# Two layers of a decoder in one program: layer 1's attentions form their scores twice, keys side by side for the maximum and keys on partitions for the exponentials

## The chip, the cores and the metric

The kernel runs on one core of one Trainium2 chip, as one program. The time is the device time of an execution in microseconds (us). A profile is one more execution, recorded by the hardware profiler; its span runs from the first to the last instruction. The engines are PE (TensorE, with its weight loads as PEld), DVE (VectorE), ACT (ScalarE), POOL (GpSimd) and SP (SyncE, which here only issues DMAs).

## The reference, cut to what matters

32 sequences of 128 tokens with 128 features pass through two layers, all in float32. Layer 0 is a recurrent (RWKV) block, a cross attention with 16 heads of 64 features over the sequence's context and 128 memory positions, and a mixture of eight experts with two chosen per token. Layer 1 is a causal self attention with normalised queries and keys ("sa" below), a windowed cross attention ("wa") and a linear layer on values rounded to blocks of four-bit floats. Each is added to the residual stream.

```python
x = x + rwkv(layernorm(x)); x = x + cross_attention(layernorm(x), ctx); x = x + experts(layernorm(x))

# layer 1, self attention: 16 heads of 8 features
q, k = headnorm(q, gq, bq), headnorm(k, gk, bk)
scores = jnp.where(causal, einsum('nhld,nhmd->nhlm', q, k), -1e30)
x = x + einsum('nhlm,nhmd->nhld', softmax(scores), v) @ Wo.T + bo

# layer 1, windowed cross attention: 16 heads of 8 features, keys and values are ctx itself
scores = einsum('bhqd,bhkd->bhqk', layernorm(x), ctx) / sqrt(8)
scores = jnp.where(abs(i - j) > 64, -inf, scores)
x = x + einsum('bhqk,bhkd->bhqd', softmax(scores), ctx) @ W_proj.T + b_proj

x = x + quantised(layernorm(x)) @ quantised(weight).T + bias
```

The masked, full softmax of a score tile is what the change forms in another way.

## The kernel before

**Work.** The 32 sequences are cut into ten groups (`SIZES`: three of two, six of four, one of two). Layer 0 works group by group; its expert layer gathers tokens into 39 blocks of 256, of which 22 are planned with layer 0 and 17 with layer 1. Layer 1 works group by group, too: a group's self attention, then its windowed attention, then its quantised linear layer, and inside an attention sequence by sequence. There are 32 + 32 such attentions of one sequence, each with 16 heads.

**Order.** Nothing is issued directly. Each operation is recorded with its engine, a weight (its estimated length in us), what it reads and writes, and a due time `at`. `Plan.run` then plays the program through as a list of events: an engine that comes free takes, of its operations that are ready and find room in their rings of buffers, the one that is due first. The order so found is written into each engine's instruction stream and stays fixed. `SHIFTS` holds, for each of the two layers, corrections to the due times by kind of operation. `SWITCH` is what the planner charges when PE changes its tiling. PE runs untiled for most work, split by rows for scores ("rows") and by columns for value sums ("columns").

**Layer 0, where the change touches it.** In `rwkv`, the eight scans of a group each need v and r repeated over partitions. For early groups (`early`, line 581) a matmul with `sel` makes each repeat (L640), and the eight products are summed in the matmuls of L694. For the others, v and r go to HBM and come back repeated by DMA (L646, L650), and POOL sums the products (L690). `clear` writes zeros to the 17 MB buffer `xreg` by DMA in the same stage. The cross attention's scores are L843, its transposes L865, its value sums L796.

**One attention of layer 1** (`attention`, L1307). Heads are stored 8 features each on 128 partitions; a row tile of 32 partitions holds four heads. POOL multiplies the keys by a mask of heads (`km`, L1311), so that one row tile's matmul gives four heads' scores side by side. PE first writes the causal or window mask into PSUM as an identity times a bf16 mask of 0 and -1e30 (L1317), then adds the scores of four row tiles (L1325). They stand with queries on partitions: two tiles `sc` of 128 x 1024, eight heads each. For each, DVE takes the negated maximum over keys (`nm`, L1338) and adds it (`e`, L1340), ACT takes exponentials (L1342), PE turns the eight heads by transposes (L1350), ACT copies them out of PSUM (`eT`, L1353). The value sums (L1358) need keys on partitions, which the transposes are for; values carry a column of ones, so that the sums of the exponentials come out beside them. ACT copies (`avs`), PE turns back (`ot`, L1369), DVE divides (L1376, L1377).

PSUM has eight banks of 128 x 512 floats: ring `big` of two pairs (scores, expert hidden values) and ring `one` of four single banks (all else), shared by both layers. The self attention of group g + 1 is planned ahead of the windowed attention of group g.

## Time and profile before

| | us |
|---|---|
| three timed executions | 1518.4, 1513.4, 1508.7; median 1513.4 |
| the profiled execution, its own time | 1505.7 |
| its span | 1504.0 |
| PE busy, share of the span | 1387.6, 92% |
| DVE busy | 1227.2, 82% |
| ACT busy | 967.9, 64% |
| POOL busy | 697.5, 46% |
| granted PE clock, mean | 0.982 |

Layer 0's attentions take about the first 815 us, the expert blocks the time to about 985, layer 1's attentions the rest. Busy time is the time in which an engine had at least one instruction under way. Matmuls are pipelined and their ends are modelled, so that a matmul's duration is longer than the time by which it delays the next one. A group of instructions stands in the profile with its source line, engine, operation, output and inputs, their shapes, the count, the total and the mean duration, and what ended the engine's idle time before it. Shares of busy time are means over stages with different limits; the prediction reads them stage by stage.

### The profile page before, as it was taken

The numbers are of one execution on the slowest core, as the hardware profiler recorded it, in microseconds if no ns is written. First come the engines' busy times: TensorE is split into PE (matmuls) and PEld (weight loads), VectorE is DVE, ScalarE is ACT, GpSimd is POOL, SyncE is SP. The second block draws the span as 40 slices with busy tenths as digits, with TensorE's granted clock in tenths as the row PEclk, the third lists the DMA queues.
The fourth block names the chain that finished last, engine by engine and source line by source line (L and its number), as shares of the span: only waits on it lengthen the run. The fifth ranks groups of instructions, "written<-read, shape, count | busy, mean of one in ns | idle before, by whom it ended". The sixth has DMA issues, their size and how long they took to land. (4 is left out here: it accounts for less than half of the span.)

```text
span 1504.0 us, 34761 instructions
## 1 busy us (share of the span) xinstructions
PE 1387.6 (92%) x12957; PEld 1069.1 (71%) x12957; DVE 1227.2 (82%) x2688; ACT 967.9 (64%) x2423; POOL 697.5 (46%) x1010
## 2 busy tenths in 40 slices
PE   6899999999999999999998998987888989999995
PEld 4678777787887878878787887964556656566664
DVE  6899898887878868796656575689999989999996
ACT  2467656676766766565674343446777888888784
POOL 6444554543546235262303466658553552553432
PEclk9999999999999999999999998999999999999997
DMA  9903030301203112020000776823000000000000
GB/s 332 324 24 108 16 123 19 113 30 66 84 1 108 43 63 86 2 79 5 16 2 24 230 210 177 252 81 88 15 12 12 19 12 12 16 8 19 5 9 18
DMA packets 80504, 107.64 MB, mean 72 GB/s; under 512 B 7152, under 2 KB 48624, under 8 KB 80336
## 3 DMA queue, kind: packets, MB, share of 16 engines
q1 hardware_dynamic: 75792, 95.97, 20.3%
q0 software_dynamic: 4544, 9.45, 1.8%
q8 instruction: 103, 1.69, 0.5%
q14 instruction: 65, 0.53, 0.1%
HBM read 73.01 MB, written 32.38 MB: 70 GB/s over the span
## 5 line engine op out<-in xcount | busy, mean ns | idle before, releaser
L855 ACT ACTIVATE e<-sc,nm 128x256 f32<-128x256 f32 x512 | 238.3, 482 | 26.1 <-DVE nm L848 26.0
L848 DVE TENSOR_REDUCE nm<-sc 128x4 f32<-128x1024 f32 x128 | 154.6, 1216 | 26.7 <-PE sc L843 25.8
L865 PE MATMUL tr<-ident,e 128*128 128x128 f32 x1024 | 144.0, 278 | 8.7 <-DVE xoT L816 7.5
L865 PEld LDWEIGHTS tr<-ident,e 128*128 128x128 f32 x1024 | 114.4, 142 | 40.6 <-issue 18.9
L1162 ACT ACTIVATE hT<-h_ps,wb 128x256 f32<-128x256 f32 x156 | 65.6, 470 | 94.2 <-PE h_ps L1159 77.4
L805 POOL COPY wide<-xrs 128x512 f32<-128x512 f32 (+1 forms) x80 | 49.0, 614 | 156.9 <-DVE xrs L803 59.9
L843 PE MATMUL sc<-xk,xq 64*128 64x128 f32 x1024 | 112.2, 296 | 0.0
L690 POOL TENSOR_TENSOR r<-r,r 128x512 f32<-128x512 f32 (+1 forms) x49 | 60.3, 1230 | 111.5 <-DVE r L688 98.7
L869 ACT COPY eT<-tr 128x512 f32<-128x512 f32 x128 | 75.3, 588 | 54.5 <-PE tr L865 50.5
L855 ACT ACTIVATION_READ_ACCUMULATOR e<-sc,nm 128x1 f32 x512 | 109.2, 213 | 0.0
L796 PE MATMUL av<-eT,xv 128*64 128x128 f32 x1024 | 104.1, 282 | 0.4 <-DVE xv L778 0.2
L1183 POOL DMA_INDIRECT ytok<-rw,bk_at x78 | 76.9, 986 | 54.5 <-DVE xT L1134 24.6
L843 PE MATMUL sc<-mkT,xq 64*128 64x128 f32 x1024 | 99.9, 272 | 0.0
L796 PE MATMUL av<-eT,mvx 128*64 128x128 f32 x1024 | 99.9, 274 | 0.0
L843 PEld LDWEIGHTS sc<-xk,xq 64*128 64x128 f32 x1024 | 77.9, 187 | 25.5 <-issue 20.7
L871 DVE COPY eT<-tr 128x512 f32<-128x512 f32 x128 | 86.1, 675 | 7.5 <-PE tr L865 7.0
L684 DVE TENSOR_TENSOR_SCAN s<-dec,v 128x512 f32<-128x512 f32 (+1 forms) x80 | 87.1, 1094 | 1.1
L766 ACT COPY xk<-xk_ps 128x512 f32<-128x512 f32 (+1 forms) x80 | 40.0, 501 | 72.3 <-PE xk_ps L764 67.5
L1340 DVE TENSOR_TENSOR e_sa<-sc_sa,nm_sa 128x1024 f32<-128x1024 f32 x64 | 78.4, 1225 | 6.9 <-ACT ff_xn L506 0.5
L816 DVE TENSOR_TENSOR xoT<-av,overs 128x512 f32<-128x512 f32 (+1 forms) x80 | 46.3, 578 | 45.7 <-PE av L796 40.2
L1340 DVE TENSOR_TENSOR e_wa<-sc_wa,nm_wa 128x1024 f32<-128x1024 f32 x64 | 78.4, 1225 | 6.2 <-DVE nm_wa L1338 0.5
L1338 DVE TENSOR_REDUCE nm_sa<-sc_sa 128x8 f32<-128x1024 f32 x64 | 77.8, 1215 | 6.3 <-PE sc_sa L1325 5.6
(586 smaller groups left out, 3932.0 us busy)
## 6 DMA issues: line engine op xcount, KB each, us to landing
xreg<-zero SPq DMA_DIRECT2D x8, 2112.0 KB
v<-spill_v SPq DMA_DIRECT2D x48, 256.0 KB
r<-spill_r SPq DMA_DIRECT2D x48, 256.0 KB
wk<-in_wexp SPq DMA_DIRECT2D x8, 512.0 KB
wq<-in_wexp SPq DMA_DIRECT2D x8, 512.0 KB
wv<-in_wexp SPq DMA_DIRECT2D x8, 512.0 KB
mkT<-in_wexp SPq DMA_DIRECT2D x8, 512.0 KB
mvx<-in_wexp SPq DMA_DIRECT2D x7, 512.0 KB
```

What stands on the lines that cost most here:

```text
L684: V(1.34, lambda u=u, s=s: vec.tensor_tensor_scan(s(), flat(dec()), u(), 0.0, ALU.mult, ALU.add), [dec, u], [s, ("scan", (g, j))])
L796: pe.matmul(av()[r, b], mvx[:, 2 * c + par] if half else v()[:, b, r], eTs[b // 2]()[:, par, half, b % 2], start=(half == 0), stop=(half = ...
L843: pe.matmul(sc()[:, par, at : at + T], q()[r, b0 + b], mkT[r, c] if half else k()[r, b0 + b], start=True, stop=True)
L848: V(1.22, lambda: vec.tensor_reduce(nm(), sc().rearrange("p j (b k) -> p j b k", k=2 * T), AX.X, ALU.max, negate=True), [sc], [nm])
L855: act.activation(e()[:, par, b], sc()[:, par, b * 2 * T : (b + 1) * 2 * T] .rearrange("p (c k) -> p c k", k=T), AF.Exp, bias=nm()[:, par, ...
L865: pe.transpose(tr()[:, half, b], e()[:, par, b, half], ident)
L869: A(0.6, lambda tr=tr: act.copy(eT()[:, 1], tr()), [tr], [(eT, 1)])
L871: V(0.68, lambda tr=tr: vec.tensor_copy(eT()[:, 0], tr()), [tr], [(eT, 0)])
L1162: A(0.47, lambda f=f: act.activation(hT()[:, f], hid(f), AF.Gelu, bias=wb()[:, f : f + 1]), [(h_ps, f % 2), wb] + ["exp"] * (j < BLK1), [( ...
L1183: d = pool.indirect_dma_start(out=ytok, out_offset=bass.IndirectOffsetOnAxis(ap=at()[:, c : c + 1], axis=0), in_=yr()[:, c], in_offset=None)
L1338: V(1.22, lambda nm=nm, sc=sc: vec.tensor_reduce(nm(), sc(), AX.X, ALU.max, negate=True), [scs[half]], [nm])
L1340: V(1.22, lambda nm=nm, sc=sc, e=e: vec.tensor_add(e(), sc(), bc(nm(), T)), [scs[half], nm], [e])
```

## The change

In layer 1, scores are formed twice. The first scores are as before, and DVE takes the negated maxima from them (`nm`, now one tile of four row tiles with 32 columns each). The maxima are split into a bf16 part and its remainder, transposed once (`nT`) and spread over four heads by a mask (`nx`, bf16). Then the scores are formed again with the keys as the stationary side, so that keys stand on partitions: a matmul of ones with `nx` writes the negative maximum into PSUM, and the keys times the masked queries (`qm`, made on ACT) are added (`st`). ACT takes the exponentials straight from PSUM into `eT`. The mask of the reference is applied after that, by POOL: `affine_select` sets the exponentials outside the causal or window region to zero. The subtraction on DVE, the sixteen transposes and the four copies are gone.

Around it, the PSUM rings belong to the layers: layer 0 keeps two pairs and four single banks, layer 1 has three pairs and two single banks. Self attentions are planned two groups ahead of the windowed ones, with four value buffers instead of three. In layer 0, group 2 is no longer early. The planner may hold PE to its present tiling: among ready operations due within `keep` of the first, one in the present mode goes first (`KEEP`, 1.3 in layer 0, none in layer 1). All shifts of due times are new.

```diff
--- before.py
+++ after.py
@@ -30,6 +30,7 @@
 assert sum(SIZES) == NB
 H, DH = 16, 8
 XH, XD = 16, 64
+VP = 32
 E, FF = 8, 512
 NF = FF // P
 NEG = -1e30
@@ -72,52 +73,45 @@
 
 
 SHIFTS = [{
-    "ACT cen#ps# cen#": 0.09, "ACT cen#ps# sq#": -0.22, "ACT g#ps# gate#": -1.15, "ACT h#ps# wb#": 0.6,
...
+    "ACT": -0.66, "ACT cen#ps# cen#": 0.78, "ACT dd#ps# dd#": -0.98, "ACT g#ps# gate#": 1.41,
...
+    "DVE xr# bk#which#": 1.05, "DVE xsm# xrs#": -0.48, "DVE xv#ps# xv#": -0.32, "KEEP": 1.3,
...
 }, {
...
 }]
@@ -150,8 +144,7 @@
     HANDOVER = {("PE", "ACT"): 0.2, ("PE", "DVE"): 0.2, ("DVE", "PE"): 0.13, ("DVE", "ACT"): 0.17,
                 ("DVE", "POOL"): 0.2, ("ACT", "DVE"): 0.07, ("ACT", "POOL"): 0.15, ("POOL", "DVE"): 0.05}
 
-
-    SWITCH, KEEP = 0.13, 0.0
+    SWITCH = 0.13
 
     def __init__(self, shifts):
         self.ops, self.seen, self.at, self.size, self.shifts = [], {}, 0.0, 1.0, shifts
@@ -194,6 +187,8 @@
         free_at = dict.fromkeys(engines, 0.0)
         room, events, order, t = {}, [], [], 0.0
         turns, modes = {}, dict.fromkeys(engines)
+
+        keep = abs(self.shifts.get("KEEP", 0.0))
         for o in self.ops:
             banks = [x for x in o[4] if x.pool.space == PSUM]
             for x in o[4]:
@@ -215,8 +210,17 @@
                 for e in engines:
                     if free_at[e] > t + 1e-9:
                         continue
-                    for k, (_, i) in enumerate(ready[e]):
+                    other = None
+                    for k, (at, i) in enumerate([*ready[e], (math.inf, None)]):
+                        if other is not None and at > ready[e][other][0] + keep:
+                            k, other = other, -1
+                            i = ready[e][k][1]
+                        if i is None:
+                            break
                         if ready_at[i] > t + 1e-9:
+                            continue
+                        change = keep and self.ops[i][7] != modes[e]
+                        if change and other is not None and other >= 0:
                             continue
                         new = {x: None for x in self.ops[i][4] if not x.held}
                         for x in list(new):
@@ -228,6 +232,9 @@
                             continue
                         if any(q in turns and max(turns[q][x] for x in xs) >= given[q] + len(xs)
                                for q, xs in need.items()):
+                            continue
+                        if change and other is None:
+                            other = k
                             continue
                         for q, xs in need.items():
                             room[q] -= len(xs)
@@ -280,13 +287,13 @@
     vec, act, pool, pe, sync = nc.vector, nc.scalar, nc.gpsimd, nc.tensor, nc.sync
 
     const = ctx.enter_context(tc.tile_pool(name="const", bufs=1))
-    ps_big = ctx.enter_context(tc.tile_pool(name="ps_big", bufs=2, space=PSUM))
-    ps_one = ctx.enter_context(tc.tile_pool(name="ps_one", bufs=4, space=PSUM))
-
     loads = []
 
 
     layer0 = ExitStack()
+    ps_big = layer0.enter_context(tc.tile_pool(name="ps_big", bufs=2, space=PSUM))
+    ps_one = layer0.enter_context(tc.tile_pool(name="ps_one", bufs=4, space=PSUM))
+    BIGS = [2, 4]
     const0 = layer0.enter_context(tc.tile_pool(name="const0", bufs=1))
 
     def load(name, shape, src, at=0.0, pool=const):
@@ -343,7 +350,12 @@
 
     hq = const.tile([P, 4], F32, tag="hq", name="hq")
     vec.tensor_reduce(hq, hm.rearrange("p (r i) -> p i r", i=4), AX.X, ALU.add)
+
+    hm8 = const.tile([P, 4], F32, tag="hm8", name="hm8")
     hqs = const.tile([P, 4], F32, tag="hqs", name="hqs")
+    vec.tensor_reduce(hm8, ident.rearrange("p (r c) -> p c r", c=VP)[:, 0:4], AX.X, ALU.add)
+    vec.tensor_reduce(hqs, ident.rearrange("p (r c) -> p c r", c=VP)[:, 4:8], AX.X, ALU.add)
+    vec.tensor_add(hm8, hm8, hqs)
     vec.tensor_scalar_mul(hqs, hq, 1.0 / math.sqrt(DH))
 
     hmp = const.tile([P, H], F32, tag="hmp", name="hmp")
@@ -450,10 +462,10 @@
         plan.op("SP", weight, fn, r, w, land)
 
     def big(name):
-        return Ring(ps_big, "big", 2, [P, 2, 512], name)
+        return Ring(ps_big, "big", BIGS[0], [P, 2, 512], name)
 
     def one(shape, name):
-        return Ring(ps_one, "one", 4, shape, name)
+        return Ring(ps_one, "one", BIGS[1], shape, name)
 
     def xk(g):
         return f"x{g}"
@@ -578,7 +590,7 @@
     def rwkv(g):
         start, n = plan.at, SIZES[g]
 
-        early = g < 3
+        early = g < 2
 
         def w(i):
             return rw[:, i, :]
@@ -1222,8 +1234,7 @@
 
     LEAD = 2
     RG = 4
-    VP = 32
-    NVX = 3
+    NVX = 4
 
     def centre_qk():
 
@@ -1236,7 +1247,7 @@
                                                   start=True, stop=True), [t], [ps2])
             V(0.2, lambda w=w, ps2=ps2: vec.tensor_copy(w, ps2()), [ps2], ["wqkv"])
 
-    vxs = []
+    vxs, nm_tiles, batches = [], [], []
 
     def pad_values():
 
@@ -1249,6 +1260,10 @@
                 pool.memset(t[:, :, :, DH : DH + 1], 1.0)
 
             G(3.0, fill, [], [f"vx16_{i}"])
+        for i in range(3):
+            t = work.tile([P, RG, VP], F32, tag=f"nmw{i}", bufs=1, name=f"nmw{i}")
+            nm_tiles.append(t)
+            G(0.3, lambda t=t: pool.memset(t, 0.0), [], [f"nmw_{i}"])
 
     def prepare_sa(g, n):
         xnT = turned(g, normal(g, "sa"), same, f"sa_xnT{g}", "xnT")
@@ -1305,11 +1320,19 @@
         return xnT, cT, hqs, vx, vkey, band
 
     def attention(m, b, qT, kT, headmask, vx, vkey, mask, o):
+
+
         n = plan.at
         plan.at = n - 1.2
-        km = wt([P, 4, T], "km", f"km{m}")
+        km, qm = (wt([P, 4, T], i, f"{i}{m}", 3) for i in ("km", "qm"))
         G(1.05, lambda: pool.tensor_mul(km(), kT()[:, b].unsqueeze(1).to_broadcast([P, 4, T]),
                                         bc(headmask, T)), [kT], [km])
+
+        def mask_q():
+            for i in range(4):
+                act.activation(qm()[:, i], qT()[:, b], AF.Copy, scale=headmask[:, i : i + 1])
+
+        A(1.4, mask_q, [qT], [qm])
         scs = [big(f"sc16_{m}_{half}") for half in range(2)]
         for half in range(2):
             def masks(half=half):
@@ -1326,31 +1349,59 @@
                           start=False, stop=True)
 
         M(0.9, scores, [qT, km], scs, "rows")
+
+        turn = len(batches)
+        batches.append(m)
+        nm, hi = turns("nm16", nm_tiles, turn), sm([P, RG, 4], "hi16", f"hi16_{m}", 3, BF16)
+        for half in range(2):
+            V(1.22, lambda half=half: vec.tensor_reduce(
+                nm()[:, 2 * half : 2 * half + 2, 0:4], scs[half]().rearrange("p j (h k) -> p j h k", k=T),
+                AX.X, ALU.max, negate=True), [scs[half]], [(nm, half)] + [f"nmw_{turn % 3}"] * (turn < 3))
+
+        def split():
+            vec.tensor_copy(hi(), nm()[:, :, 0:4])
+            vec.tensor_sub(nm()[:, :, 4:8], nm()[:, :, 0:4], hi())
+
+        V(0.4, split, [], [nm, hi])
+        nT = one([P, T], f"nT{m}")
+        M(0.14, lambda: pe.transpose(nT(), nm().rearrange("p r c -> p (r c)"), ident), [nm], [nT])
+        nx = wt([P, 4, T], "nx", f"nx{m}", 3, BF16)
+        V(0.69, lambda: vec.tensor_mul(nx(), nT().unsqueeze(1).to_broadcast([P, 4, T]), bc(hm8, T)), [nT], [nx])
+        plan.at = n - 0.5
+        sts = [big(f"st16_{m}_{half}") for half in range(2)]
+
+        def scores_turned():
+            for r in range(RG):
+                rows = slice(VP * r, VP * (r + 1))
+                pe.matmul(sts[r // 2]()[:, r % 2], ones16[rows], nx()[rows].rearrange("p h q -> p (h q)"),
+                          start=True, stop=False)
+            for r in range(RG):
+                rows = slice(VP * r, VP * (r + 1))
+                pe.matmul(sts[r // 2]()[:, r % 2], kT()[rows, b], qm()[rows].rearrange("p h q -> p (h q)"),
+                          start=False, stop=True)
+
+        M(1.15, scores_turned, [kT, qm, nx], sts, "rows")
         av = one([P, 4, T], f"av16_{m}")
         eTs = []
         for half in range(2):
-            def sc(half=half):
-                return scs[half]().rearrange("p j (h k) -> p (j h) k", k=T)
-
-            plan.at = n - 1.2
-            nm = sm([P, 8], "nm16", f"nm16_{m}_{half}")
-            e = wt([P, 8, T], "e16", f"e16_{m}_{half}", 4)
-            V(1.22, lambda nm=nm, sc=sc: vec.tensor_reduce(nm(), sc(), AX.X, ALU.max, negate=True),
-              [scs[half]], [nm])
-            V(1.22, lambda nm=nm, sc=sc, e=e: vec.tensor_add(e(), sc(), bc(nm(), T)), [scs[half], nm], [e])
-            plan.at = n - 0.5
-            A(1.06, lambda e=e: act.activation(e(), e(), AF.Exp), ["gelu"], [e])
-            eT = wt([P, 8, T], "eT16", f"eT16_{m}_{half}", 4)
+            eT = wt([P, 8, T], "eT16", f"eT16_{m}_{half}", 6)
             eTs.append(eT)
-            for j in range(2):
-                tr = one([P, 4, T], f"tr16_{m}_{half}_{j}")
-
-                def turn(j=j, tr=tr, e=e):
-                    for i in range(4):
-                        pe.transpose(tr()[:, i], e()[:, 4 * j + i], ident)
-
-                M(0.44, turn, [e], [tr])
-                A(0.6, lambda j=j, tr=tr, eT=eT: act.copy(eT()[:, 4 * j : 4 * j + 4], tr()), [tr], [(eT, j)])
+            A(1.06, lambda half=half, eT=eT: act.activation(
+                eT().rearrange("p h q -> p (h q)"), sts[half]().rearrange("p j n -> p (j n)"), AF.Exp),
+              [sts[half], "gelu"], [eT])
+
+            def select(eT=eT):
+
+                if mask is causal:
+                    pool.affine_select(out=eT(), in_=eT(), pattern=[[0, 8], [1, T]], compare_op=ALU.is_ge,
+                                       fill=0.0, base=0, channel_multiplier=-1)
+                    return
+                for q0, sign in ((0, 1), (WINDOW, -1)):
+                    part = eT()[:, :, q0 : q0 + WINDOW]
+                    pool.affine_select(out=part, in_=part, pattern=[[0, 8], [sign, WINDOW]], compare_op=ALU.is_ge,
+                                       fill=0.0, base=WINDOW + sign * q0, channel_multiplier=-sign)
+
+            G(1.1 if mask is causal else 1.3, select, [], [eT])
 
         def attend():
             for h in range(H):
@@ -1489,18 +1540,21 @@
     layer0.close()
 
     plan = Plan(SHIFTS[1])
-    with tc.tile_pool(name="small1", bufs=1) as small, tc.tile_pool(name="work1", bufs=1) as work:
+    BIGS[:] = 3, 2
+    with (tc.tile_pool(name="ps_big1", bufs=3, space=PSUM) as ps_big,
+          tc.tile_pool(name="ps_one1", bufs=2, space=PSUM) as ps_one,
+          tc.tile_pool(name="small1", bufs=1) as small, tc.tile_pool(name="work1", bufs=1) as work):
         def tiles_of(name, j, shape):
-            return wt(shape, "xT", f"xT{j}") if name == "xT" else wt(shape, "eT16", f"hT{j}", 4)
+            return wt(shape, "xT", f"xT{j}") if name == "xT" else wt(shape, "eT16", f"hT{j}", 6)
 
         BLK_AT[0] = 0.5
         for j in range(BLK1, NBLK):
             expert_block(j, -NBLK * BLK_AT[0] - 8)
         plan.at = -12
         pad_values()
-        jobs = [("sa", 0)]
+        jobs = [("sa", 0), ("sa", 1)]
         for g in range(NG):
-            jobs += [("sa", g + 1)] * (g + 1 < NG) + [("wa", g)]
+            jobs += [("sa", g + 2)] * (g + 2 < NG) + [("wa", g)]
         n = 0
         for i, (tag, g) in enumerate(jobs):
             if tag == "sa":
```


## The prediction

> **What bounds the kernel now.** I read the timeline in 40 slices first, then busy time in stretches, then the groups of instructions by shape, and last the order of time on single engines.
>
> ```profile
> PE   6899999999999999999998998987888989999995
> DVE  6899898887878868796656575689999989999996
> POOL 6444554543546235262303466658553552553432
> ```
>
> Slices are 37.6 us. Layer 0 fills the first 21, the expert blocks follow to about 985 us, and layer 1's attentions take the last 13 or so. PE is full nearly throughout; DVE is as full only in the last part.
>
> ```profile
> core 0: us, PE busy (x) PEld busy (x) DVE busy (x) ACT busy (x) POOL busy (x), PEclk, DMA share, GB/s
> 0.00:50.00 50.00, 33.27 (x139) 25.22 (x140) 35.18 (x101) 13.18 (x33) 30.19 (x73) 0.97 0.99 345
> 50.00:100.00 50.00, 47.61 (x315) 36.89 (x314) 45.79 (x112) 27.05 (x87) 18.04 (x27) 1.00 0.44 148
> ...
> 150.00:790.00 640.00, 626.31 (x6066) 502.84 (x6065) 511.81 (x1024) 422.23 (x1290) 270.42 (x360) 1.00 0.15 50
> 1280.00:1394.00 114.00, 106.22 (x1146) 72.37 (x1142) 105.48 (x167) 93.34 (x165) 52.42 (x69) 1.00 0.05 14
> ```
>
> The third row is layer 0's steady state: PE 97.9% busy, nobody else above 80%, so PE's work is its time. The fourth is 16 attentions of layer 1 in steady state (two sa groups, two wa groups, 57 us each): PE 106.2 and DVE 105.5 of 114 us. Two engines share the bound, and the chain of waits there runs mostly over DVE's maximum and subtraction. POOL has 61.6 us free.
>
> ```profile
> L1340 DVE TENSOR_TENSOR e_wa<-sc_wa,nm_wa 128x1024 f32<-128x1024 f32 x64 | 78.4, 1225 | 6.2 <-DVE nm_wa L1338 0.5
> L1338 DVE TENSOR_REDUCE nm_wa<-sc_wa 128x8 f32<-128x1024 f32 x64 | 77.8, 1216 | 3.4 <-PE sc_wa L1325 3.4
> L1353 ACT COPY eT_wa<-tr_wa 128x512 f32<-128x512 f32 x128 | 68.7, 592 | 18.8 <-PE tr_wa L1350 18.3
> L1342 ACT ACTIVATE e_wa<-e_wa 128x1024 f32<-128x1024 f32 x64 | 67.2, 1064 | 5.5 <-DVE e_wa L1340 4.9
> L1311 POOL TENSOR_TENSOR kmwa<-wa_ctxT,hqs 128x512 f32<-128x512 f32 x32 | 33.3, 1042 | 77.8 <-PE sc_sa L1325 33.8 <-issue 25.4 <-PE sc_wa L1325 18.6
> L1401 POOL TENSOR_SCALAR fx_t<-fx_t 128x512 f32<-128x512 f32 x6 | 3.7, 613 | 0.5
> ```
>
> These price an attention: two maxima and two subtractions on DVE are 2 x (1.216 + 1.225) = 4.88 us.
>
> ```profile
> 1340.91 1.04 PE L1350 MATMUL tr_sa<-ident,e_sa 128*128 128x128 f32 x8
> 1341.88 1.08 PE L1358 MATMUL av_sa<-eT_sa,vx 128*32 128x128 f32 x32
> 1342.93 0.59 PE L1317 MATMUL sc_wa<-band,ident 128*128 128x512 bf16 x2
> 1343.45 1.14 PE L1325 MATMUL sc_wa<-kmwa,wa_xnT 32*128 32x512 f32 x8
> 1344.52 0.66 PE L1369 MATMUL otsa<-ident,avssa 128*128 128x128 f32 x4
> ```
>
> On PE starts are what counts, because an end overlaps the next start. Eight transposes take 0.97 us to the next start, 0.10 of it a change from whole-array to tiled matmuls, so one costs 0.107. Two mask matmuls take 0.52, with a change, so 0.21 each. Eight score pieces take 1.07, with a change: four row tiles run side by side, 0.85 of streaming and about 0.1 for the first weights. In layer 0, four transposes stand 0.43 apart from the next block of whole-array work and 0.53 from a tiled one: again 0.10 a change.
>
> **The change, part by part.** *Layer 0, fewer repeats on PE.* Group 2 no longer repeats v and r by matmul (16 of 128x256) and sums its eight products on POOL instead of in the matmul (7 fewer). Such a matmul is two instructions, 0.43 us start to start in that stage: 23 x 0.43 = 9.9 us off PE. Added are 2 stores and 16 loads of 128 KB on SP's queue, and 7 POOL sums of 128x256 at 0.73 (the bias add of that shape), 5.1 us on an engine 42% busy. The loads queue behind the 17 MB of clearing, which keeps DMA at 0.99 of the first 50 us and is over by about 75; in the changed order group 2's projections stand among group 0's cross attention, which covers the wait. Uncovered, it is bounded by the 4 to 9 us that group 3's loads spread over now.
>
> *Layer 0, another order.* All due times are new and PE now may prefer an operation of its present tiling for up to 1.3 us. Counting tiling changes in the two instruction orders: 388 before, 307 after, 81 x 0.10 = 8.1 us. PE's 18.0 us together are worth their length only where PE is full; in the first 100 us it is 81% busy, and most of the repeats lie there. I take 16; bounds 20 and 0.
>
> *Layer 1, DVE.* Per attention the two subtractions (2.45) go. Added are a split of the 128x16 maxima in two small operations (the reciprocal of that shape has 0.24, so 0.5) and one 128x512 product out of PSUM (the residual add of that shape has 0.68). Net -1.27, over 16 attentions -20.3: 105.5 to 85.2.
>
> *Layer 1, PE.* Out go 16 transposes, 1.71. In come the second scores, 0.85 as the first; the bf16 rank-one pass that subtracts the maximum, 0.21 if its four row tiles run side by side as the score pieces do (0.85 if one after the other, as four masks do; nothing like it is in the trace, and the score pieces in the same tiling are nearest, so 0.21); one transpose, 0.11. Net -0.54. Changes of tiling rise from 242 to 333 in layer 1, +0.14 an attention, and 63 more entries into row tiles expose first weights, +0.10. Sum -0.29, over 16 attentions 106.2 to 101.5. If the rank-one pass runs serially, +10.2: 111.7.
>
> The Trainium skill (TensorEngine Tiling (Array Packing), Key Properties) says that changing the tiling mode drains the array, which speaks against layer 1's 91 extra changes. The rows price that drain at 0.10 us, 9.1 us in layer 1 against 8.1 saved in layer 0; the page gives no price.
>
> *Layer 1, ACT.* Four copies (4 x 0.592) go; four scaled copies of 128x128 come. The value copy of that shape has 0.28, the normalisation with two pointers 0.49, four in 1.65: so 1.1 to 1.65, I take 1.4. The exponentials keep 1.06, now out of PSUM. Net -1.0, 93.3 to 78 of 114: off the path.
>
> *Layer 1, POOL.* Each attention's two exponential tiles are masked here, in POOL's queue among the q/k normalisation (1.9 us pieces), bias adds (1.27) and quantisation, and the value matmuls wait for it. The trace has the operation only at 128x128 (0.28) and 128x16 (0.19) in the setup, some 0.9 ns a column, hence about 1.1 for 1024. The other one-input row, the clamp L1401, has 0.613 for 512. The two-input km product at 1.04 for 512 is the upper bound. It has one input, so I take the clamp: 2 x 1.13 causal, 4 x 0.613 band, mean 2.36; over 16 attentions +37.7, 52.4 to 90.1. Upper bound 4.17 an attention, 119.
>
> The Trainium skill (GPSIMD Engine Reference, Engine selection and the side-by-side cycle accounting) advises against elementwise work on this engine and gives a tight loop 768 ns for 512 elements; by it POOL has 49 us more, 101.5, level with PE, and half of layer 1's gain is gone. The clamp's measured 0.613 disagrees.
>
> *Layer 1, order and buffers.* PSUM becomes three score pairs and two single banks (two and four before). A score pair was held through maximum and subtraction, 1.9 us of PE and up to 4.9 of DVE; now through the maxima only, but a second set follows it. The single banks serve everything else, and a late nT, av or ot holds half of them. The sa groups run two ahead of wa rather than one. The chain of one attention grows: from 1.22 + 1.23 + 1.06 + 1.04 + 0.59 = 5.1 us behind its last scores to 1.22 + 0.5 + 0.3 + 0.68 + 1.35 + 2.13 + 1.13 = 7.3. Neighbours hide that in the steady state; at filling and draining it shows, +4 together.
>
> *The sum.* In layer 1 PE's 101.5 us is the longest, then POOL's 90.1, DVE's 85.2 and ACT's 78. Now PE is 93.2% busy with a second engine as full; in layer 0 it reaches 97.9% with the next at 80%. POOL will stand at 84%. I take 94.5%: 107.4, -6.6 per 114 us. The steady state lasts 1010 to 1480, 4.12 such stretches: -27. With layer 0's -16 and the ends' +4 that is -39. The profiled execution took 1505.7 us (span 1504.0), giving 1467; the median of the three runs is 7.7 above it, and against that median I say 1474.
>
> **The rivals.** *Everything tighter* (0.12): PE reaches layer 0's 97.9% (103.7, -42), layer 0 gives its 20, and the order two groups ahead removes some of PE's 20 idle us between 1000 and 1100, say 10 net of the ends. 1513 - 72 = 1441. For it: DVE is relieved most there. Against it: POOL is 64% busy there before any masks.
>
> *Layer 1 stands still* (0.12): two single banks and the longer chain make PE wait as much as it saves. Only -16 + 4 is left, 1501. For it: one value sum or a transposed maximum held late blocks every transposition behind it. Against it: about 7 us of holding an attention over two banks is 3.7 of a 6.7 us period.
>
> *Layer 0's gain is lost* (0.05): the new order leaves gaps where the old one had none; 1490.
>
> *POOL becomes the bound* (0.13): masking costs its upper bound, 4.17 an attention; POOL needs 119 us of each 114, at 95% busy 125, +11 x 4.12 = +45, less 16, plus 4: 1546, slower. It decides from (0.95 x 114 - 52.4) / 16 = 3.5 us an attention, 0.87 per 512 columns. For it: queue order, and every value matmul behind POOL. Against it: both one-input rows lie well below.
>
> **How the numbers follow.** The forecast has 0.58; its own range is PE at 97.9% or at today's 93.2% in layer 1 (-42 or -21) with 20 or 10 in layer 0: 1455 to 1486. The range of 8 in 10, 1446 to 1515, leaves out POOL's case and half of the tighter one. A measurement here tells about 1% (15 us) from no change. Faster by more: forecast, tighter, most of the lost layer 0 and a quarter of standing still, 0.77; within: 0.10; slower: 0.13.
>
> **What would show it.** Right: layer 0's steady stretch ends some 15 us earlier with PE still near 98%; 16 attentions take 105 to 109 us with DVE near 80% and POOL near 85%; masking is 1.1 to 1.3 us a tile; the rank-one pass is about 0.21 start to start. Wrong: the mask's group above 1.75 us a tile, value matmuls idling for POOL by several us per attention, PE under 90% in the last third, or 0.85 us for the rank-one pass.

## The result, and the profile after

The changed kernel takes 1518.7 us (median of 20 runs, 1512.9 to 1527.8) against 1514.5 for the kernel before beside it: a ratio of 1.0034, 95% interval 1.002 to 1.0047. The forecast was 1474, and its range ended at 1515. The profiled execution took 1521.8 us, its span 1520.1.

The timeline in 40 slices (38.0 us each) of the changed kernel, the same three rows as before:

```profile
PE   6899989999999999999998997978788889987995
DVE  6899889997978798785655664686697887887776
POOL 6445474454536453342313656668877677777665
```

In the last third DVE is relieved, as forecast, and POOL filled. PE, which was to run into the room, falls from nines to eights. In stretches, the first row is layer 0's steady state, the second 16 attentions of layer 1 (from the 65th to the 97th exponential):

```profile
core 0: us, PE busy (x) PEld busy (x) DVE busy (x) ACT busy (x) POOL busy (x), PEclk, DMA share, GB/s
150.00:790.00 640.00, 621.74 (x6036) 506.52 (x6034) 515.74 (x1042) 414.75 (x1268) 286.75 (x370) 0.99 0.15 50
1286.59:1399.17 112.58, 98.57 (x1031) 50.95 (x1030) 91.69 (x182) 74.01 (x152) 85.01 (x117) 0.98 0.05 14
```

PE's work did shrink in this stretch, to 98.6 us for 16 attentions (101.5 forecast, 106.2 before). But 112.6 us pass in place of the 107.4 forecast: PE is 88% busy, where 94.5% had been taken, and no other engine is above 82%. The groups of layer 1 by shape (busy us, mean ns; then the idle time before them) give the prices:

```profile
L1401 POOL TENSOR_SCALAR_AFFINE_SELECT eT_wa<-eT_wa 128x512 f32<-128x512 f32 x128 | 83.3, 685 | 29.9 <-ACT eT_wa L1389 29.5
L1396 POOL TENSOR_SCALAR_AFFINE_SELECT eT_sa<-eT_sa 128x1024 f32<-128x1024 f32 x64 | 68.8, 1097 | 16.1 <-ACT eT_sa L1389 15.8
L1333 ACT ACTIVATE qmsa<-qkT,hq 128x128 f32<-128x128 f32 x128 | 40.6, 392 | 29.9 <-PE st_sa L1380 19.3 <-PE st_wa L1380 10.7
L1369 DVE TENSOR_TENSOR nxsa<-nTsa,hm 128x512 bf16<-128x512 f32 x32 | 21.7, 680 | 4.3 <-PE nTsa L1367 4.1
L1362 DVE CAST hi_sa<-nmw 128x16 bf16<-128x16 f32 x32 | 13.3, 416 | 0.1
L1363 DVE TENSOR_TENSOR nmw<-nmw,hi_sa 128x16 f32<-128x16 f32 x32 | 12.2, 381 | 1.1
```

The masks on POOL cost what was forecast. The last two lines do not fit: 128x16 takes 0.4 us on average and 0.14 at its fastest. One such instruction in the timeline, all engines in order of start:

```profile
1308.21 1.90 POOL L1289 TENSOR_TENSOR qk_sq<-qk 128x1024 f32<-128x1024 f32 x1
1308.50 1.64 DVE L1362 CAST hi_wa<-nmw 128x16 bf16<-128x16 f32 x1
...
1310.17 0.18 DVE L1363 TENSOR_TENSOR nmw<-nmw,hi_wa 128x16 f32<-128x16 f32 x1
...
1310.34 0.68 DVE L1369 TENSOR_TENSOR nxsa<-nTsa,hm 128x512 bf16<-128x512 f32 x1
...
1311.17 0.60 PE L1409 MATMUL av_wa<-eT_wa,vx 128*32 128x128 f32 x13 [0.72 <-DVE nxsa L1369]
```

The cast starts 0.3 us into a POOL product of 1.90 and ends with it (1310.14 and 1310.11). The product `nxsa` queues behind it. It is what frees `nTsa`, one of the two single PSUM banks, and PE's next value sum, which needs a bank, stands for 0.72 us. In the changed kernel 37 of the split's 128 instructions last over 0.3 us; each of the 37 ends within 0.12 us of the end of a POOL instruction, and together they lose 23.5 us. Eleven others began and ended inside a POOL instruction without waiting, ten of them beside POOL's power step on 128x2 or 128x4 (L499, 0.7 to 1.0 us): not every POOL instruction holds DVE up. Instructions on DVE that read PSUM, and reductions, differ by at most 65 ns within a group of one shape.

The Trainium skill has this as a rule (SBUF — State Buffer, "SBUF: two separate sides"): DVE and POOL share a pair of SBUF ports under an exclusive lock, for DVE operations in a two-port mode or with two SBUF inputs, and whoever comes second waits for the whole instruction of the other. The 37 ends agree with it; why the eleven did not wait stays open. The rule spoke against this change, and the prediction did not weigh it.

### The profile page after: what moved, and what is told of

It reads as the page before. It is cut to its first block, busy times and chain, and to the rows that moved or that the text cites. A ratio compares the mean times of both kernels' runs of the same rounds, so it can differ in the third digit from the quotient of the medians.

```text
span 1520.1 us, 34373 instructions
## 1 busy us (share of the span) xinstructions
PE 1372.0 (90%) x12719; PEld 1001.2 (66%) x12719; DVE 1168.5 (77%) x2755; ACT 904.9 (60%) x2423; POOL 866.9 (57%) x1214
## 5 line engine op out<-in xcount | busy, mean ns | idle before, releaser
L877 PEld LDWEIGHTS tr<-ident,e 128*128 128x128 f32 x1024 | 118.0, 142 | 34.2 <-issue 18.5
L817 POOL COPY wide<-xrs 128x512 f32<-128x512 f32 (+1 forms) x80 | 52.9, 662 | 145.7 <-DVE xrs L815 84.8
L702 POOL TENSOR_TENSOR r<-r,r 128x512 f32<-128x512 f32 (+1 forms) x56 | 69.5, 1242 | 78.1 <-DVE r L700 70.2
L808 PE MATMUL av<-eT,mvx 128*64 128x128 f32 x1024 | 103.1, 278 | 0.0
L1401 POOL TENSOR_SCALAR_AFFINE_SELECT eT_wa<-eT_wa 128x512 f32<-128x512 f32 x128 | 83.3, 685 | 29.9 <-ACT eT_wa L1389 29.5
L1357 DVE TENSOR_REDUCE nmw<-sc_wa 128x8 f32<-128x1024 f32 x64 | 76.0, 1217 | 28.4 <-PE sc_wa L1348 28.0
L696 DVE TENSOR_TENSOR_SCAN s<-dec,v 128x512 f32<-128x512 f32 (+1 forms) x80 | 92.1, 1155 | 1.1
L1357 DVE TENSOR_REDUCE nmw<-sc_sa 128x8 f32<-128x1024 f32 x64 | 75.5, 1213 | 11.9 <-PE sc_sa L1348 11.1
L855 PEld LDWEIGHTS sc<-mkT,xq 64*128 64x128 f32 x1024 | 79.2, 189 | 1.0 <-issue 1.0
```

The lines of the kernel that those rows point to most:

```text
L696: V(1.34, lambda u=u, s=s: vec.tensor_tensor_scan(s(), flat(dec()), u(), 0.0, ALU.mult, ALU.add), [dec, u], [s, ("scan", (g, j))])
L702: G(1.35, lambda o=o, q=outs[j - 1]: pool.tensor_add(o(), o(), q()), [outs[j - 1]], [o])
L808: pe.matmul(av()[r, b], mvx[:, 2 * c + par] if half else v()[:, b, r], eTs[b // 2]()[:, par, half, b % 2], start=(half == 0), stop=(half = ...
L855: pe.matmul(sc()[:, par, at : at + T], q()[r, b0 + b], mkT[r, c] if half else k()[r, b0 + b], start=True, stop=True)
L877: pe.transpose(tr()[:, half, b], e()[:, par, b, half], ident)
L1357: V(1.22, lambda half=half: vec.tensor_reduce(nm()[:, 2 * half : 2 * half + 2, 0:4], scs[half]().rearrange("p j (h k) -> p j h k", k=T), A ...
```

## The experiments

All ratios are to the kernel before, run beside it on the same chip; 0.001 is 1.5 us. The changed kernel stands at 1.0034. For each profile I read three stretches from the order of time: from the end of the last expert product to the first exponential of layer 1 ("fill"), to the start of the last exponential ("run"), to the end of the span ("drain"). "Layer 1" below means the three together; these are its rows in the changed kernel and in e1, with the columns as above:

```profile
1000.40:1520.10 519.70, 432.76 (x4378) 223.43 (x4376) 402.72 (x871) 319.77 (x670) 384.05 (x505) 0.95 0.07 20
997.90:1499.60 501.70, 434.93 (x4559) 291.18 (x4556) 452.67 (x793) 377.26 (x663) 233.49 (x312) 0.97 0.07 20
```

| kernel | ratio, 95% interval | fill, run, drain us |
|---|---|---|
| before | 1 | 6.2, 470.5, 25.3 |
| changed | 1.0034 (1.002 to 1.0047) | 26.6, 464.4, 28.7 |
| e1 layer 0 alone | 0.9913 (0.9893 to 0.9933) | 6.2, 470.3, 25.1 |
| e2 layer 1 alone | 1.0097 (1.0076 to 1.0118) | 26.3, 462.9, 28.8 |
| e3 no split, other order | 1.0134 (1.0111 to 1.0157) | 26.5, 471.2, 36.5 |
| e4 small selections | 0.9893 (0.9867 to 0.9919) | 26.5, 443.9, 26.0 |
| e5 no split, same order | 0.9913 (0.9898 to 0.9928) | 26.8, 458.4, 28.4 |
| e6 replanned | 1.0007 (0.9993 to 1.0021) | 20.5, 469.7, 27.4 |
| e7 no split, replanned | 0.9864 (0.9846 to 0.9881) | 20.2, 440.9, 29.3 |
| e8 old layer 1, POOL load | 1.0239 (1.0222 to 1.0256) | 8.5, 516.6, 25.3 |
| e9 split twice | 1.0233 (1.0211 to 1.0255) | 27.0, 496.2, 28.1 |
| e10 as e5, one execution | 0.994 | 26.6, 450.0, 26.8 |
| e11 e7 one ahead | 0.9918 (0.990 to 0.9937) | 21.4, 450.0, 24.8 |
| e12 maximum over all keys | 0.9758 (0.9737 to 0.9779) | 18.5, 426.1, 27.4 |
| e13 no split, small selections | 0.9835 (0.9819 to 0.985) | 26.6, 439.9, 27.0 |
| e14 e12, three groups on DVE | 0.9679 (0.9664 to 0.9694) | 7.4, 426.1, 31.4 |

**Which layer: e1 and e2.** e1 gives the kernel before the changed layer 0 (due times, `KEEP`, `early = g < 2`), e2 the changed kernel the old layer 0.

> The kernel before with layer 0 of the change alone (its due times, the preference for the present tiling, group 2's repeats on matmul gone); layer 1 and its buffers as before. The prediction gave layer 0 -16 us. In the profiled execution of the change the last value sum of layer 0 is 7 us earlier and the first expert matmul 11.3 us earlier, but the expert blocks then take 104.0 us in place of 93.4 up to the boundary of the layers. Theory 1 (the gain of layer 0 is real and is given back in its own expert blocks, whose order came out worse): -1 us, within 3 of no change. Theory 2 (the expert blocks were slow by an accident of that one execution, and the gain carries through): -8 to -11 us. Theory 3 (the prediction): -16 us.

> Layer 0 as before, layer 1 as changed. If layer 0 is worth nothing at the end (theory 1), this shows the whole difference of the changed kernel, +4 us by the medians (+15 by the two profiled executions). If layer 0 carries -8 to -11 us through (theory 2), layer 1 alone is +12 to +15 us. The prediction had layer 1 at -23 us. In its profile the first exponential should again be about 19 us later than before, counted from the last expert block.

Layer 0 is worth -13.2 us and carries through: theory 2, by somewhat more than its range, and near the forecast's -16. Layer 1 alone costs +14.7. Theory 1, read from the pair of profiles, falls. Beside each other on one chip e1's first expert matmul is 19.8 us earlier than e2's (819.3 against 839.1), its last expert product 11.1 us (997.9 against 1009.0): the expert blocks take 178.6 us in e1 and 169.9 in e2, so theory 1's mechanism is there, but gives back only 8.7 us. With equal layer 0, changed against e1, layer 1 is +20.4 in the fill, -5.9 in the run and +3.6 in the drain, +18.1; by the ratios +18.3.

**The split: e5, e9, e10, and e3's accident.** For e5 the split is emptied; its place in every order stays. The maximum rounded to bf16 is then the shift, exact after the normalisation.

```diff
-        V(0.4, split, [], [nm, hi])
+        V(0.4, lambda: None, [], [nm, hi])
-    vec.tensor_add(hm8, hm8, hqs)
```

> As e3_no_split, but with the due time of the split kept for the empty step, so that every engine's order is that of the changed kernel with the two small DVE operations left out. e3 had lost that due time, its order differed, and it took 15 us more than the changed kernel although DVE had 37 us less to do. Theory A (the two small operations, 0.72 us an attention with their waits for POOL, sit in the serial chain): -10 to -20 us against the changed kernel's 1518.7. Theory B (buffers): -0 to -5. Theory D (the order decides, and e3's loss was its changed order): also -10 to -20 here, since with the order kept nothing is against the saving; a time above 1518 would say that the split itself was never in the way.

e9 issues the two instructions twice:

> The changed kernel with the split's two small operations issued twice, everything else and every order kept. In ratios to the kernel before, the changed kernel stands at 1.0034 and the one without the split at 0.9913 (e5), 18 us lower. Theory A (the two operations are on the path, at their measured 0.67 us start to start with the waits for POOL): doubling costs as much as leaving out saved, +12 to +25 us, ratio 1.011 to 1.020. Theory D' (e5 gained by luck of the order): +0 to +6 us, ratio under 1.008.

e5 lies 18.3 us below the changed kernel, e9 30.1 above. Both agree with theory A, e9 beyond its range: in e9 DVE's busy time in layer 1 rises by 28 us (403 to 431) and all of it is paid, so the split is on the path. e10 is e5's kernel once more:

> e5 once more in one look, to have its profile from the chip of this call beside e9: 1495 to 1503 us.

It took 1510.7 us, on a chip where the kernel before took 1520.4; the absolute number missed, the sign did not. It is also the better profile: e5's profiled execution was the slowest of its six (1503.0 us, median 1495.6) and its layer 1 only 6.1 us shorter than the changed kernel's; e10's is 16.3 us shorter, 14.4 of them in the run. e3 had been meant as e5, but its empty step named only `nm`, not `hi`:

> The changed kernel without the split of the maxima: the bf16 product with hm8 takes the maximum's rounding to bf16 as the shift, which is the same for every key of a query and so cancels in the normalised result; the two small DVE operations per attention go, the order of everything else is kept. Theory A (the split lies in the serial chain, and its two operations, 0.80 us measured per attention for 0.31 at their fastest, wait for running POOL instructions): about 0.8 us per attention shorter chain and 51 us less DVE time; where DVE's lateness is what PE waits for, that is worth 0.2 to 0.4 us an attention, -13 to -25 us. Theory B (PE waits for buffers: the single banks and the score pairs are held too long whatever DVE does): -0 to -5 us. Theory C (POOL sets the pace in the first 90 us of layer 1 and the order does in the rest): -5 us, none of it before 1100 us.

With `hi` the step lost its due time (4.39 for sa, -1.28 for wa), and the planner put out another order: with DVE 30 us shorter (403 to 373) it was 15 us slower than the changed kernel. All three theories missed. These two due times are worth more (33 us between e3 and e5) than any term of the prediction.

**The selections: e4 and e13.** Each selection covers 2 columns per head instead of 128 or 64.

```diff
-                    pool.affine_select(out=eT(), in_=eT(), pattern=[[0, 8], [1, T]], ...
+                    pool.affine_select(out=eT()[:, :, 0:2], in_=eT()[:, :, 0:2], pattern=[[0, 8], [1, 2]], ...
```

> The changed kernel with each selection cut to 2 of the 128 or 64 columns per head, so most exponentials stay unmasked and the results are not the reference's; instructions, waits and order are kept, POOL loses about 2.0 us per attention, 130 us in all. Theory A (DVE's small operations wait for running POOL instructions): the mean of the cast falls from 0.37 to about 0.25 and of the subtraction from 0.35 to about 0.25, other small DVE operations get shorter too, -15 to -25 us, spread over the whole of layer 1. Theory B (buffers): only the 1 to 1.3 us of chain per attention goes, -3 to -8 us. Theory C (POOL sets the pace from 1010 to 1100 us): -10 to -15 us, nearly all before 1100 us.

-21.4 us, spread over the whole run (fill unchanged), with the split's instructions shorter. Groups of e4 by shape:

```profile
L1362 DVE CAST hi_sa<-nmw 128x16 bf16<-128x16 f32 x32 | 9.4, 293 | 0.1
L1362 DVE CAST hi_wa<-nmw 128x16 bf16<-128x16 f32 x32 | 9.1, 283 | 0.2
```

416 and 327 ns before the cut: theory A. DVE loses 32 us in layer 1 (403 to 371), of which 12 are the split's. Waits of over 0.3 us fall from 37 to 19, and again every one ends with a POOL instruction. To see whether that is all, e13 leaves out split and selections together:

> The changed kernel without the split and with each selection cut to 2 columns per head (most exponentials stay unmasked), every order kept. Alone, the first gave a ratio of 0.9913 and the second 0.9893, against 1.0034 for the changed kernel. One cause (the selections cost time because the split's operations wait for them): together no more than the larger alone, 0.985 to 0.991. Two causes (the split as a step of the chain, the selections as a step of it and as load in POOL's queue): their sum, 1.0034 less 0.0121 less 0.0141, 0.977, within 0.973 to 0.981.

It lies 30.1 us below the changed kernel, between the ranges of the two theories: more than either alone (21.4 and 18.3), less than their sum (39.7). So the two share some 10 us. The split's waits that e4 removed (23.5 to 11.6 us) have that size; that they are the shared part is not shown. The rest of the selections' 21 us is their own. How much of that is the other small DVE operations and how much the step in the chain these runs don't part.

**POOL's load by itself: e8.** Old layer 1, with two selections of 128x1024 on an unused tile behind every km product.

> Layer 0 of the change with layer 1 as before (1502.2 us in e1), and behind every km product on POOL two selections of 128x1024 on a tile that nobody reads: about 2.2 us more of POOL work per attention, 140 us in all, as much as the change adds, but in no chain. Theory A (a busy POOL by itself stretches DVE's small operations): per-line means of the variance, offset and quantiser steps rise as in the changed kernel, and the attention's own maximum, subtraction and normalisation, which read PSUM, do not; +2 to +8 us. Theory C (POOL's load as such, through its queue): +15 to +20 us, as much as the changed layer 1 loses against the old one.

Per line the first half came true. Groups on DVE of e1, then of e8:

```profile
L1342 DVE TENSOR_TENSOR e_wa<-sc_wa,nm_wa 128x1024 f32<-128x1024 f32 x64 | 78.4, 1225 | 6.2 <-DVE nm_wa L1340 0.5
L517 DVE TENSOR_SCALAR qk_y<-qk_var 128x128 int32<-128x128 int32 x6 | 1.4, 227 | 0.2
L490 DVE SCALAR_TENSOR_TENSOR ff_off<-ff_mv,ff_rstd 128x4 f32<-128x4 f32 x6 | 0.9, 154 | 1.2 <-POOL ff_rstd L489 1.2
```

```profile
L1347 DVE TENSOR_TENSOR e_wa<-sc_wa,nm_wa 128x1024 f32<-128x1024 f32 x64 | 78.4, 1225 | 6.2 <-DVE nm_wa L1345 0.5
L517 DVE TENSOR_SCALAR qk_y<-qk_var 128x128 int32<-128x128 int32 x6 | 3.8, 626 | 0.2
L490 DVE SCALAR_TENSOR_TENSOR ff_off<-ff_mv,ff_rstd 128x4 f32<-128x4 f32 x6 | 3.7, 621 | 1.2 <-POOL ff_rstd L489 1.2
```

The subtraction that reads PSUM does not move by a nanosecond, the operations between SBUF tiles take three to four times as long. But DVE's total in layer 1 rises by only 24 us (453 to 477), and the kernel by 49 against e1, two and a half times theory C's upper bound of 20. POOL work put in at one place, into an order made without it, costs more than the whole new layer 1; a busy share of about 70% did not tell that. PE's waits from 990 us on grow from 63.6 us in e1 to 100.2 in e8: by 14 for DVE's subtractions, by 13 for POOL's quantised values (`fx_t`), by 8 for ACT's normalised values (`wa_xn`). Why these come later in this order stays open.

**Order and buffers: e6, e7, e11.** For e6 the planner's durations of DVE steps are corrected to measured ones, and layer 1's due times searched anew; the instructions stay.

```diff
+    "DVE nm# hi#sa#": (0.0, 0.67), "DVE nm# hi#wa#": (0.0, 0.67), "DVE ff#xn# fx#amax#": (1.25, 0.0),
+    "DVE fx#t# fx#c#": (1.5, 0.0), "DVE fx#c# fx#t#": (1.35, 0.0), "DVE qk#sq# qk#var#": (1.2, 0.0),
...
-    plan = Plan(SHIFTS[1])
+    plan = Plan(SHIFTS[1], COSTS)
```

> The changed kernel, same instructions in layer 1, but the planner is told the measured DVE durations (the split 0.67 instead of 0.40, the quantiser's steps 1.2 to 1.5 times as long, 0.1 more for the variance and offset steps) and layer 1's due times were searched anew against these. Theory D (layer 1 lost because its planned order rested on durations that DVE doesn't keep while POOL runs): -10 to -20 us against 1518.7, so 1499 to 1509, part of it in the first exponential coming earlier. Theory B (the buffers and the longer chain make PE wait in any order): within 4 us of 1518.7. DVE's small operations should stay as long as they are in the changed kernel in either case.

> e6 without the split of the maxima, due times searched for that. If e5 and e6 both gain, this should gain most of both: 1490 to 1500 us, faster than layer 0 of the change alone (1502.2). If only one of them is a real cause, it equals that one. If neither, 1515 to 1520.

e6 gains 4.1 us, at the edge of what theory B allowed and far from D: this other order hardly mends it while the split is there. e7 gains 25.7, about as much as e5 and e6 together (22.4), and beats layer 0 alone. In one stretch of 100 us PE gets what the forecast had taken for granted:

```profile
1200.00:1300.00 100.00, 95.60 (x1049) 50.69 (x1042) 78.66 (x138) 76.35 (x165) 85.99 (x115) 1.00 0.06 16
```

The changed kernel has 88.99 us there, with the same two single banks. But this is one of e7's best stretches: over its whole run PE is 88.6% busy, against 86.6 in the changed kernel and 90.0 in e1. What PE waits for tells more. In layer 1 it stands for 81.7 us in the changed kernel, 51.4 of them until a DVE result; in e10 DVE's part is 39.1, in e7 31.2, in e9 72.2. So late DVE results behind the same number of buffers are a large part of PE's waiting. No run of the new layer 1 has another number of banks, so what the two single banks cost by themselves isn't shown.

> e7 with the sa groups one ahead of the wa groups, as before the change, instead of two; due times searched for that. In the changed kernel the first exponential comes 26.6 us after the last expert block's second product, against 6.2 with the old layer 1; e6 and e7 still have 20. Theory E (the order two groups ahead costs those 20 us and they are lost): first exponential within 10 us, and 5 to 15 us faster than e7 (ratio 0.977 to 0.983). Theory F (the two-ahead order only moves work: what stands before the first exponential is missing later): same as e7 or slower, ratio 0.985 to 0.992.

Theory F: 8 us slower than e7, and the fill is as long (21.4). Going two groups ahead is not what delays the first exponential. (e6, e7, e11, e12 and e14 each have due times searched for them. e3 and e5 differ by two due times and by 33 us, so a difference of 8 or 16 us between kernels with different due times is partly one of orders.)

**What else the second scores allow: e12 and e14.** Once POOL hides the keys behind the exponential, the maximum needs no mask; e12 drops the mask matmuls of the first scores.

```diff
-            M(0.45, masks, [qT, kT], [scs[half]])
...
-                          start=False, stop=True)
+                          start=True, stop=True)
```

> e7 without the mask matmuls of the first scores: the maximum is taken over all keys, visible or not, which is only a shift and cancels in the normalisation as long as no hidden score exceeds the best visible one by some 80; POOL's masking of the exponentials alone hides the keys. Due times searched for it. PE loses four 128x512 matmuls, 0.21 each, 0.96 with the change of tiling per attention, about 55 us in all, and the chain starts earlier. Theory G (PE is still what layer 1 waits for): -25 to -40 us against e7, ratio 0.960 to 0.970. Theory H (POOL and the DVE chain are the bound by now): -0 to -10 us, ratio above 0.980.

-16 us against e7, between G and H: PE is not the only limit by then, as far as two different orders can tell.

> e12 with the q/k normalisation and the residual sums of a third group of 4 on DVE instead of POOL, due times searched for it. e12 stood at 0.9758. If POOL's load in the first 150 us of layer 1 (83 to 87% busy in e12) holds the filling, the 33rd exponential, 151 us after the last expert block's second product in e12 and 133 in the old layer 1, comes 5 to 10 us earlier and the ratio falls to 0.969 to 0.973. If the filling is the longer chain of an attention itself, it stays at 0.974 to 0.978.

0.9679, 12 us below e12 and the fastest of all, though not for the reason given: the 33rd exponential comes 152.1 us after the last expert product (151.4 in e12), and the gain lies later (the 97th after 350.1 against 360.2). POOL's early load does not hold the filling. The first exponential, now after 7.4 us, is no measure of it either: the 33rd, with which the 17th attention begins, comes after 163.0 us in the changed kernel, 149.9 to 162.0 in e5, e6, e7, e11, e12 and e13, and 137.9 in e1 (the 133 in the expectation was a miscount).

## Why the prediction was wrong, by its own steps

*The sum*: -39 was forecast, about +5 measured. Of the 44 us between them 3 lie in layer 0, 21 in the run of layer 1, 20 at its ends.

*Layer 0* (-16): right, -13.2 by e1, and PE is 97.1% busy over 150 to 790 us. Part of the agreement is luck: layer 0 up to the first expert matmul gained 19.8 us, nearly the upper bound of 20, and the expert blocks, which the forecast left out, took 8.7 back.

*The prices in layer 1*: right where the engine works alone. The masks cost 68.8 / 32 = 2.15 us in a causal attention and 83.3 / 32 = 2.60 in a banded one, a mean of 2.38 for 2.36 taken; four scaled copies 40.6 / 32 = 1.27 for 1.4; the product 0.68; the rank-one pass 0.23 start to start for 0.21; POOL needs 85.0 us for 16 attentions for 90.1. (The setup's two rows give 0.8 ns a column, not 0.9; a tile of 1024 measured 1.08.) The Trainium skill's 768 ns for 512 elements (GPSIMD Engine Reference, the side-by-side cycle accounting) lies above the 83.3 / 128 = 651 that a band mask of that size takes here.

*The split* (0.5 taken): the row it was priced by, a reciprocal of 128x16, reads PSUM and does not wait for POOL. Before and after the change:

```profile
L1376 DVE RECIPROCAL rs_sa<-otsa 128x16 f32<-128x16 f32 x32 | 7.7, 241 | 0.8 <-PE otsa L1369 0.8
L1427 DVE RECIPROCAL rs_sa<-otsa 128x16 f32<-128x16 f32 x32 | 7.8, 245 | 20.6 <-PE otsa L1420 20.6
```

The split measured 0.72 busy. DVE has 91.7 us for 16 attentions in place of 85.2, and the other small operations between SBUF tiles grew too. The step that failed first was to add work to POOL and work of the exposed kind to DVE and to price each alone.

*"I take 94.5%"*: one of the two steps that cost most, 21 us. The share was put between layer 0's and today's by counting busy engines. But the chain maximum, split, transposition, product, second scores holds one of two single banks and a score pair, and what delays it delays PE: 88%. In place of -27 the run gave -5.9. Of the prediction's signs of being wrong one came, PE under 90% in the last third. e5 and e9 show that the split did a large part of it; e4 and e13 that the selections do as well. PE's work is a second part: 0.29 an attention less would be 18.6 us over all 64, but from the last expert product on PE is busy 432.8 us against 434.9 in e1, and its mean clock is 0.95 against 0.97 (see the last section).

*"+4 together" for filling and draining*: 24.0 by the three stretches, the other step, 20 us. The chain's extra 2.2 us were counted once. In the changed kernel's fill, DVE is in this order (the scores were there at 1009.7):

```profile
1010.87 0.69 DVE L1298 TENSOR_TENSOR qk<-qk,qk_y 128x512 f32<-128x512 f32 x1
1011.48 2.35 DVE L1357 TENSOR_REDUCE nmw<-sc_sa 128x8 f32<-128x1024 f32 x2
1013.86 0.46 DVE L1362 CAST hi_sa<-nmw 128x16 bf16<-128x16 f32 x1
1014.36 0.96 DVE L1363 TENSOR_TENSOR nmw<-nmw,hi_sa 128x16 f32<-128x16 f32 x1
1015.82 2.36 DVE L1357 TENSOR_REDUCE nmw<-sc_sa 128x8 f32<-128x1024 f32 x2 [0.49 <-PE sc_sa L1348]
1018.09 0.68 DVE L1369 TENSOR_TENSOR nxsa<-nTsa,hm 128x512 bf16<-128x512 f32 x1
```

The second group's normalisation stands ahead of the first maximum, the second attention's maxima ahead of the first product. That is one order's story, and e14 shows that another first exponential does not save the time up to the 33rd. Neither the split (e5), nor the selections (e13), nor the order (e6, e7), nor the masks (e12) brings the 33rd exponential back to 137.9; 12 to 24 us are left in each. The clock is a part of it, by an estimate from two rows at most 9 us: over the first 118 us of layer 1 it is 0.88 in the changed kernel and 0.96 in e1. What holds the rest stays open.

*The rivals.* "Layer 1 stands still" named a part of the mechanism, a transposed maximum held late in one of two single banks (of PE's 81.7 us of waiting in layer 1, 13.5 end with the product that frees it and 16.9 with a maximum), and nearly the right size for the run; it had 0.12 and left out the fill. "POOL becomes the bound" did not occur by its price (2.38 against 3.5), yet POOL's load did much of the harm without being the bound, in part through DVE. No rival had that.

## What to carry to other kernels

Work moved to POOL is not free because POOL has room: look for DVE's small operations from SBUF to SBUF, compare their mean with their fastest, and see whether the long ones end with a POOL instruction. Where two such operations sit in a serial chain that holds scarce buffers, remove them before anything else; here the shift of a softmax needed only one rounding, and its maximum no mask. And an engine's busy share in one stage is no estimate of what it reaches in another with a longer chain.

## What the runs showed of the hardware

A DVE cast of 128x16 takes 0.14 us at its fastest and up to 1.64 behind a POOL product; a DVE subtraction of 128x1024 out of PSUM takes 1225 ns in e1 and in e8 alike, with POOL 43% and 69% busy from 1100 to 1480 us.

The granted TensorE clock falls to half for a few us at a time, after a stretch in which PE had gaps. Three stretches of the changed kernel:

```profile
1002.19:1005.60 3.41, 0.92 (x7) 0.52 (x6) 3.10 (x11) 0.94 (x5) 2.08 (x3) 1.00 0.12 41
1005.60:1009.02 3.42, 3.42 (x12) 1.17 (x13) 3.25 (x6) 3.29 (x10) 2.03 (x2) 0.50 0.39 111
1108.10:1370.80 262.70, 230.30 (x2389) 117.58 (x2389) 216.62 (x440) 173.70 (x365) 200.46 (x262) 1.00 0.05 14
```

In the 3.4 us before each of the 16 times that the clock falls in this profile, PE is busy at most 0.64 of the time. The Trainium skill (TensorE: Matmul & The Clock Gate, Part 1) says the clock is halved after an idle stretch of some 3.4 us and comes back with activity; the rows agree with the halving and the length, but here PE did not have to be idle throughout.

Two things follow for this case. From 1108 to 1371 us the clock is full, and PE is busy only 88% all the same: there its waits are what is missing, not the clock. But a wait can cost twice. In layer 1 the clock is at half for 53.7 us in the changed kernel and for 28.6 in e1; half of the difference, some 12 us of the 18 by which the new layer 1 loses to the old one, is an estimate of what the slower PE cost at most. The 20 executions of the changed kernel agree in size: from 0.964 (1526.1 us) to 0.975 (1516.7 us) of mean clock, a straight line through all of them gives some 12 us for 0.01, and the medians are 0.969 for the changed kernel and 0.98 for e1. No run changes the clock by itself, so this stays an estimate.
